# A transformer block with a Fourier layer on one core: two token tiles normalised on another engine, and the last sums of the MLP in three pieces

## The chip, the cores and the metric

The kernel runs on one core of a Trainium2 chip. The metric is the device time of one execution in microseconds; of the kernel before there are three runs, 2810.19, 2811.89 and 2812.22 us, median 2811.89 us. One more execution was recorded by the hardware profiler; every duration below is from it. The engines have short names in the profile: PE (TensorE, matrix products), PEld (its weight loads), DVE (VectorE), ACT (ScalarE), POOL (GpSimd) and SP (SyncE, which here only issues transfers). Each engine takes its own instructions in a fixed order; between engines, semaphores say when an operand is there.

## The reference

The input is x, 48 x 48 positions of 768 channels, which are 2304 tokens. Layer 0 is a transformer block, cut here to what matters:

```python
xn = layernorm(x, ln1_g, ln1_b)
qkv = xn @ qkv_w + qkv_b
out = softmax(q k^T * scale + rel_h + rel_w) v @ proj_w + proj_b     # 12 heads
x = x + out
xn2 = layernorm(x, ln2_g, ln2_b)
h = gelu(xn2 @ mlp_w1 + mlp_b1)                                      # 3072 wide
x = x + (h @ mlp_w2 + mlp_b2)
```

Layer 1 takes a two-dimensional Fourier transform of x over the 48 x 48 positions, multiplies the modes with small complex weights (8 blocks of 96 channels) in two steps with relu and soft shrinkage, transforms back and adds x. All data are float32.

## The kernel before

A tile of tokens is 128 tokens (one for each partition) by 768 channels; there are 18 of them. The stages follow each other on PE: layer norm and the products for q, k and v; attention; the projection; the MLP; the Fourier layer.

**The start.** `arrive(g)` loads three token tiles into one buffer `x3` (L403 to L406, one transfer on SP for each tile). Before the first product the first six tiles are normalised in place. `look_at(t)` (L410) takes mean and variance on DVE (two `bn_stats` L414, one `bn_aggr` L416) and the square root of the variance on ACT (L418). `normal(t)` (L421) takes the reciprocal on DVE (L424) and then, also on DVE, subtracts the mean and multiplies by the reciprocal (L426). The loop at L635 to L642 sets the order by hand for DVE, ACT and POOL: look at 0, look at 1, normalise 0, look at 2, normalise 1, normalise 2. Then `channels_first(0)` (L504) transposes the three tiles on PE (L510, in the order tile 0, 1, 2 for every 128 channels), scales them on DVE (L513) and ACT (L517), and PE goes on to the first products `plain_queries_and_keys` (L574). The load of the second set of weights (`weights_of` with `normalised[0]`, L379) is held back until tile 0 is normalised. Four POOL additions and subtractions (L166 to L169, from `left`) work on that load.

**The MLP.** Its products are done by Winograd's form of Strassen's scheme: seven products of half-size blocks in place of eight, at the price of sums of blocks before and after. Tokens go in three blocks `p` of 768 (two halves of G = 384), the 3072 hidden channels in 12 chunks `n` of 256 (two halves of 128). For each `(p, n)`:

- `hidden(p, n)` (L1332) makes the chunk of h: products on PE (L1343), sums on DVE (L1355), gelu on ACT (L1349). It is a generator that is advanced four times; in its last step `left` (L165 to L169) makes the sums of activations that the second product needs. With a11, a12, a21, a22 the blocks of h these are s1 = a21 + a22, s2 = s1 - a11, s4 = a12 - s2 in the buffer `hs`, and s3 = a11 - a21, which is written over a21 in `hT`. Each is one DVE instruction over 384 tokens.
- `added(p, n, i)` (L1386) makes the second product for 128 tokens of each half, i = 0, 1, 2: seven matmuls (L1408, then L1404 six times) into four PSUM banks `o0` to `o3`, each followed on DVE by an addition of the bank to `acc` or to the result in `main` (L1412 and L1406). The matmuls read, in this order, a11, s2, s3, s1, a12, a22, s4. For the last chunk of a block three more additions follow: one on DVE (L1420) and two on POOL (L1421, L1422).

In the loop at L1500 `added` of chunk n - 1 stands between the steps of `hidden` of chunk n, so that PE has products of one while DVE works for the other. After the last chunk of a block nothing of `hidden` is left: L1518 to L1521 run `added(p, 11, i)` for i = 0, 1, 2 one behind the other, for p = 0 and 1 with transposes between them (`turned`), for p = 2 with nothing between. `rows_forward(p)` (L1424) follows, the first step of the Fourier layer (L1436).

The order of PE, POOL and SP in this stage is the order in which the program issues (`in_order`), and so is that of DVE and ACT (`part_by_part`, L1497). What stands later in the text of the program stands later in the queue of its engine.

**The buffers.** `bias` (L1297) is a pool of constants that is placed ahead of the buffers for h, for the sums and for the weights.

Of the kernel before, what the change touches and what calls it, by code (L numbers as in the profile page):

```python
# [10 lines left out]
F32 = mybir.dt.float32  # L11
F32R = mybir.dt.float32r
I32 = mybir.dt.int32
AF = mybir.ActivationFunctionType
ALU = mybir.AluOpType
# [4 lines left out]
P = 128  # L20
HW = 48
T = HW * HW
# [7 lines left out]
TB = 768  # L30
G = 384
# [16 lines left out]
def block_then_afno(  # L48
# [27 lines left out]
    nc = tc.nc  # L76
# [40 lines left out]
    x1 = main.rearrange("p (t c) -> p t c", t=NT)  # L117
# [47 lines left out]
    def left(eng, a11, a12, a21, a22, s):  # L165
        eng.tensor_tensor(s[0], a21, a22, ALU.add)  # L166
        eng.tensor_tensor(s[1], s[0], a11, ALU.subtract)  # L167
        eng.tensor_tensor(s[2], a12, s[1], ALU.subtract)
        eng.tensor_tensor(a21, a11, a21, ALU.subtract)  # L169
# [30 lines left out]
    with ExitStack() as flag_scope:  # L200
# [12 lines left out]
        with ExitStack() as att:  # L213
# [121 lines left out]
            def queries_keys_values(qkv):  # L335
# [72 lines left out]
                normalised, looked_at = [], {}  # L408
# [12 lines left out]
                def normal(t):  # L421
                    x1 = arrived[t // 3][:, t % 3]
                    mv, rstd = looked_at.pop(t)
                    nc.vector.reciprocal(rstd, rstd)  # L424
                    normalised.append(
                        nc.vector.tensor_scalar(  # L426
                            x1, x1, mv[:, 0:1], rstd, ALU.subtract, ALU.mult
                        )
                    )

                def gathered(p):

# [182 lines left out]
                for p in range(T // TB):  # L615
                    work = [(0, pr) for pr in range(NC)] + [(1, i) for i in range(3)]
                    if p == 1:
                        work = work[NC:] + work[:NC]
                    elif p == 2:
                        work = work[:1] + work[NC:] + work[1:NC]  # L620
# [84 lines left out]
            with tc.manual_schedule(engines={mybir.EngineType.PE, mybir.EngineType.SP}):  # L705
# [161 lines left out]
                with tc.manual_schedule(  # L867
                    engines={mybir.EngineType.Activation, mybir.EngineType.DVE}
                ):
                    for pr in range(NC):  # L870
                        for c in range(T // G):
# [19 lines left out]
                            work = between(pr, c, acc)  # L891
# [109 lines left out]
        with tc.tile_pool(name="ps_flag", bufs=1, space=PSUM) as psum, tc.tile_pool(  # L1001
            name="ps_early", bufs=1, space=PSUM
# [55 lines left out]
        with tc.If(safe < 1):  # L1058
            with ExitStack() as att:
                xnT = main.rearrange("p (c t) -> p c t", c=NC)  # L1060
                with tc.tile_pool(name="g_ln1", bufs=3) as ln1, tc.tile_pool(
                    name="g_ps_ln1", bufs=2, space=PSUM
# [24 lines left out]
                for pr in range(NC):  # L1087
# [12 lines left out]
                    for g in range(T // G):  # L1100
                        kp = psum.tile([P, G], F32, name="g_kp", tag="m")
                        for c in range(NC):
# [5 lines left out]
                            bias=kb[0:64, pr : pr + 1], scale=HD**-0.5,  # L1108
# [18 lines left out]
                    for sg in range(T // SG):  # L1127
# [4 lines left out]
                        for i in range(2):  # L1132
                            qp = psum.tile([P, G], F32, name="qp", tag="m")
                            for c in range(NC):
# [6 lines left out]
                                bias=vec[0:64, V_QB + pr : V_QB + pr + 1],  # L1141
# [6 lines left out]
                        for i in range(2):  # L1148
                            hp = psum.tile([P, G], F32, name="g_hp", tag="m")
                            for r in range(8):  # L1150
                                h = sg * 16 + i * 8 + r
# [85 lines left out]
            with tc.tile_pool(name="g_ps_proj", bufs=2, space=PSUM) as psum, tc.tile_pool(  # L1237
                name="g_og", bufs=2
# [17 lines left out]
        with tc.tile_pool(name="ps_turn", bufs=4, space=PSUM) as psum_turn, tc.tile_pool(  # L1256
            name="ps_proj", bufs=1, space=PSUM
        ) as psum, tc.tile_pool(name="proj_late", bufs=2) as pl:
            hats, ogs = [], {EARLY: sums_of_outputs(pl, kept[EARLY])}
            for u in range(EARLY, PAIRS):  # L1260
# [5 lines left out]
                n = u - EARLY  # L1266
# [29 lines left out]
    with ExitStack() as mlp:  # L1296
# [7 lines left out]
        apart = mlp.enter_context(tc.tile_pool(name="apart", bufs=1))  # L1304
        apart.tile([P, 560], F32, name="apart")
        wpool = mlp.enter_context(tc.tile_pool(name="mlp_w", bufs=2))
        n_f = FF // FCH
        kept = {}

# [22 lines left out]
        def hidden(p, n):  # L1332

            a11, a12, a21, a22, ws, v, vs = ready_w.pop((p, n))
            h = hpool.tile([P, 2, TB], F32, name="hT")
            hs = hpool.tile([P, 3, G], F32, name="hs", bufs=1)
            kept[p, n] = h, hs, v, vs

            bank = [psum.tile([P, G], F32, name=f"h{i}") for i in range(4)]

            def product(i, a, b, start):
                for c in range(3):
                    nc.tensor.matmul(  # L1343
                        bank[i], a[:, c, :], b[:, c, :],
                        start=(start and c == 0), stop=(c == 2), skip_group_check=not start,
                    )

            def gelu(i, k, src):
                nc.scalar.activation(  # L1349
                    h[:, i, ts(k, G)], src, AF.Gelu, bias=col(V_B1 + 2 * n + i)  # L1350
                )

            def summed(src, other, name, bufs=2):
                t = upool.tile([P, G], F32, name=name, bufs=bufs)
                nc.vector.tensor_tensor(t, src, other, ALU.add)  # L1355
                return t

            b11, b21, t3, b22, t1, t2, t4 = parts_of_tokens(xt, xs)
            s1, s2, s4 = (ws[:, i] for i in range(3))
            product(0, a11, b11, True)  # L1360
            m1 = upool.tile([P, G], F32, name="m1")
            nc.scalar.copy(m1, bank[0])
            product(1, s2, t2, True)
            u = summed(bank[1], m1, "u")
            yield
            product(2, a21, t3, True)
            u7 = summed(bank[2], u, "u7")
            product(3, s1, t1, True)
            gelu(1, 1, summed(bank[3], u7, "c", 3))
            yield  # L1370
            product(0, a12, b21, False)
            gelu(0, 0, bank[0])
            product(2, a22, t4, False)
            gelu(1, 0, summed(bank[2], u, "c", 3))
            product(3, s4, b22, False)
            gelu(0, 1, summed(bank[3], u, "c", 3))
            yield
            left(
                nc.vector, h[:, 0, :G], h[:, 1, :G], h[:, 0, G:], h[:, 1, G:],
                [hs[:, i] for i in range(3)],  # L1380
            )
            yield

        acc = {}

        def added(p, n, i):  # L1386

            h, hs, v, vs = kept[p, n]
            bank = [psum.tile([P, CH], F32, name=f"o{k}") for k in range(4)]
            if n == 0:  # L1390
                acc[i] = upool.tile([P, CH], F32, name=f"acc{i}", bufs=1)
            a11, a12, s3, a22 = (
                h[:, f, ds(k * G + i * P, P)] for f, k in ((0, 0), (1, 0), (0, 1), (1, 1))
            )
            s1, s2, s4 = (hs[:, k, ts(i, P)] for k in range(3))
            b11, t3, b21, b22 = (v[:, f, ts(k, CH)] for f in range(2) for k in range(2))
            t1, t2, t4 = (vs[:, k] for k in range(3))
            t = 2 * (p * 3) + i
            x11, x12, x21, x22 = (
                x1[:, t + 3 * j, ts(k, CH)] for j in range(2) for k in range(2)  # L1400
            )

            def product(k, a, b, start, *into):
                nc.tensor.matmul(bank[k], a, b, start=start, stop=True, skip_group_check=not start)  # L1404
                for dst in into:
                    nc.vector.tensor_tensor(dst, bank[k], dst, ALU.add)  # L1406

            nc.tensor.matmul(bank[0], a11, b11, start=True, stop=True)  # L1408
            if n == 0:
                nc.vector.tensor_copy(acc[i], bank[0])  # L1410
            else:
                nc.vector.tensor_tensor(acc[i], bank[0], acc[i], ALU.add)  # L1412
            product(1, s2, t2, True, acc[i])
            product(2, s3, t3, True, x22)
            product(3, s1, t1, True, x22)
            product(0, a12, b21, False, x11)
            product(2, a22, t4, False, x21)
            product(3, s4, b22, False, x12)
            if n == n_f - 1:
                nc.vector.tensor_tensor(x21, x21, acc[i], ALU.add)  # L1420
                nc.gpsimd.tensor_tensor(x12, x12, acc[i], ALU.add)  # L1421
                nc.gpsimd.tensor_tensor(x22, x22, acc[i], ALU.add)  # L1422
# [61 lines left out]
        def turned(piece):  # L1484

            for i in range(4 * piece, 4 * piece + 4):
                j, c = divmod(i, NC)
                tp = psum.tile([P, G], F32, name="tp2", tag=f"h{i % 4}")
                for k in range(3):
                    nc.tensor.transpose(tp[:, ts(k, P)], hats[3 * j + k][:, ts(c, P)], ident)  # L1490
                nc.scalar.activation(
                    xt[:, c, ts(j, G)], tp, AF.Identity, bias=col(V_LN2B + c), scale=col(V_LN2G + c)
                )
# [6 lines left out]
        for p in range(T // TB):  # L1500
            for n in range(n_f):
                if (p, n) == (0, 2):
                    nc.sync.dma_start(out=b2, in_=mlp_b2[0, :].partition_broadcast(P))
                    nc.sync.dma_start(out=rows_dft, in_=c_rows)
                work = hidden(p, n)
                for i in range(3):
                    next(work)
                    if n:
                        added(p, n - 1, i)
                next(work)  # L1510
                if n < n_f - 1 and (p == 0 or n):
                    weights(p, n + 1)
                if p < 2 and 3 <= n < 9:
                    measured(p + 1, n - 3)
                if p < 2 and n > 8:
                    for i in range(2 * (n - 9), 2 * (n - 8)):
                        normalised(p + 1, i)
            for i in range(3):  # L1518
                if p < 2:
                    turned(i)  # L1520
                added(p, n_f - 1, i)  # L1521
            if p < 2:
                sums_of_tokens(xt, xs)
                for n in range(2):
                    weights(p + 1, n)
            rows_forward(p)
# [408 lines left out]
```

## Time and profile before

| | us |
|---|---|
| median of three runs | 2811.89 |
| the profiled execution, its own time | 2809.43 |
| its span | 2807.6 |
| PE busy | 2779.3 (99% of the span) |
| DVE busy | 1700.3 (61%) |
| ACT busy | 916.8 (33%) |
| POOL busy | 664.6 (24%) |
| first matmul starts (from the span's start) | 7.09 |
| last `added` of the MLP, first matmul | 2544.93 |
| first matmul of the last `rows_forward` | 2560.38 |

The profiled execution is 2.46 us under the median of the runs, and its span is 1.83 us under its own time. The granted clock of TensorE was 0.999 in it. A row of the timeline gives start, duration, engine, line, operation, output and inputs, shape, count, and in brackets how long the engine was idle before and what released it. Where a row has a count, the duration is that of the whole group. A matmul of float32 shows as two PE instructions in such a group.

### The profile page before, as it was taken

Reading aid. Unit: us, or ns where it says so; the run is one execution under the profiler, and the core shown is the slowest. Engines: PE = TensorE matmul, PEld = TensorE weight load, DVE = VectorE, ACT = ScalarE, POOL = GpSimd, SP = SyncE. Lnnn points to the kernel's source line nnn. Section 1 sums busy time; section 2 is a strip of 40 time slices with the busy share of each in tenths; the row PEclk is TensorE's granted clock in tenths of the full one; section 3 lists DMA queues with packets and bytes.
Section 4 is the critical chain, followed back from the end, with each engine's and each line's share of the span. In section 5 each row is a group of like instructions: output and inputs, shape, how many; then the busy total and the mean of one; then the engine's idle time right before and its main releaser. Section 6 shows DMA issues by size and latency. Waiting matters only on the chain. (4 is left out here: it accounts for less than half of the span.)

```text
span 2807.6 us, 40998 instructions
## 1 busy us (share of the span) xinstructions
PE 2779.3 (99%) x15765; PEld 1712.6 (61%) x15765; DVE 1700.3 (61%) x2504; ACT 916.8 (33%) x1457; POOL 664.6 (24%) x658
## 2 busy tenths in 40 slices
PE   8999999999999999999999999999999999999999
PEld 5555656656566566565556555555555555556888
DVE  4434245767676767676756566665666566566666
ACT  1101136656566666664501101121101211012432
POOL 2405010000000000000064332342232522322433
PEclk9999999999999999999999999999999999999999
DMA  5435385273663737546242112121121211114255
GB/s 180 160 109 168 97 158 113 56 136 66 104 129 62 132 63 120 107 73 101 84 168 79 52 67 67 45 102 57 45 68 52 97 54 63 50 56 123 64 152 158
DMA packets 218556, 269.39 MB, mean 96 GB/s; under 512 B 24772, under 2 KB 197180, under 8 KB 216816
## 3 DMA queue, kind: packets, MB, share of 16 engines
q1 hardware_dynamic: 217820, 266.15, 37.8%
q8 instruction: 127, 2.08, 0.3%
q14 instruction: 77, 0.63, 0.1%
q10 hardware_dynamic: 468, 0.33, 0.1%
q0 software_dynamic: 64, 0.20, 0.0%
HBM read 150.56 MB, written 52.32 MB: 72 GB/s over the span
## 5 line engine op out<-in xcount | busy, mean ns | idle before, releaser
L741 ACT ACTIVATE main<-sp 128x768 f32<-128x768 f32 x648 | 516.1, 812 | 34.7 <-PE sp L731 19.3
L885 DVE TENSOR_TENSOR pairs<-pairs,main 128x1536 f32<-128x1536 f32 x252 | 443.1, 1758 | 27.2 <-DVE pairs L885 0.9
L731 PE MATMUL sp<-terms,select 64*128 64x384 f32 x1296 | 412.0, 629 | 0.0
L1406 DVE TENSOR_TENSOR main<-o,main 128x384 f32<-128x384 f32 x540 | 299.7, 557 | 42.8 <-PE o L1404 0.5
L1343 PE MATMUL h<-shared,w 128*128 128x384 f32 x864 | 296.6, 486 | 0.7 <-POOL w2s L172 0.7
L722 PE MATMUL sp<-shared 64*128 64x384 f32 x1296 | 265.2, 485 | 1.6 <-ACT row_hi L246 1.0
L722 PE MATMUL sp<-qT,kT 64*128 64x384 f32 x1296 | 264.1, 484 | 0.0
L1343 PEld LDWEIGHTS h<-shared,w 128*128 128x128 f32 x864 | 163.9, 190 | 116.2 <-POOL w2s L172 1.3
L787 POOL TENSOR_TENSOR inverse<-inverse,rden 24x32 f32<-24x32 f32 x36 | 14.9, 415 | 925.8 <-DVE sums L786 886.5
L1343 PE MATMUL h<-shared,w1s 128*128 128x384 f32 x648 | 226.7, 486 | 0.0
L754 PE MATMUL op<-main,shared 128*64 128x384 f32 x1296 | 217.4, 488 | 0.0
L754 PE MATMUL op<-main,v 128*64 128x384 f32 x1296 | 216.4, 488 | 0.0
L1349 ACT ACTIVATE hT<-c,vec 128x384 f32<-128x384 f32 x108 | 66.4, 615 | 457.6 <-DVE c L1355 457.6
L885 DVE TENSOR_TENSOR pairs<-main 128x1536 f32<-128x1536 f32 x36 | 63.3, 1759 | 247.0 <-ACT main L741 247.0
L1355 DVE TENSOR_TENSOR c<-h,u 128x384 f32<-128x384 f32 x108 | 60.2, 558 | 218.4 <-PE h L1343 218.4
L731 PEld LDWEIGHTS sp<-terms,select 64*128 64x128 f32 x1296 | 125.3, 186 | 83.8
L1404 PE MATMUL o<-w2s,hs 128*128 128x384 f32 x432 | 174.9, 487 | 1.2 <-DVE hs L167 1.2
L1404 PE MATMUL o<-w,hT 128*128 128x384 f32 x432 | 175.1, 487 | 0.8 <-DVE hT L169 0.5
L1343 PEld LDWEIGHTS h<-shared,w1s 128*128 128x128 f32 x648 | 123.1, 190 | 85.9
L172 POOL TENSOR_TENSOR w2s<-w 128x384 f32<-128x384 f32 x36 | 36.0, 999 | 575.4 <-DMA w<-in_mlp_w_dram 347.2
L754 PEld LDWEIGHTS op<-main,v 128*64 128x64 f32 x1296 | 96.9, 137 | 92.7 <-issue 67.7
L553 PE MATMUL m<-main 128*128 128x384 f32 x462 | 150.6, 487 | 0.6 <-POOL main L167 0.6
(222 smaller groups left out, 4119.5 us busy)
## 6 DMA issues: line engine op xcount, KB each, us to landing
w<-in_mlp_w_dram SPq DMA_DIRECT2D x72, 768.0 KB
terms<-col_parts SPq DMA_DIRECT2D x432, 72.0 KB
terms<-row_hi SPq DMA_DIRECT2D x216, 72.0 KB
terms<-row_lo SPq DMA_DIRECT2D x216, 72.0 KB
main<-in_qkv_w_dram SPq DMA_DIRECT2D x36, 384.0 KB
z<-zt SPq DMA_DIRECT2D x48, 192.0 KB
x<-in_x_blocks_dram SPq DMA_DIRECT2D x18, 384.0 KB
q_d<-o SPq DMA_DIRECT2D x36, 192.0 KB
```

The lines of the kernel that those rows point to most:

```text
L172: eng.tensor_tensor(t[0], b12, b11, ALU.subtract)
L553: nc.tensor.matmul(bank, a[:, c, :], b[:, c, :], start=(first and c == 0), stop=(c == 2), skip_group_check=not first,)
L722: nc.tensor.matmul(sp[:, j, :G], kT[at, ts(kt, P)], qT[at, ts(c, G)], start=first, stop=not first,)
L731: nc.tensor.matmul(sp[:, j, :G], select[at, a % 2], ready[pr, c][at, a // 2, b], start=first, stop=not first,)
L741: nc.scalar.activation(p, sp[:, :, :G], AF.Exp, scale=HD**-0.5)
L754: nc.tensor.matmul(op[ts(j, 64)], v[:, kt, ts(j, 64)], exps[:, kt, j, :], start=(kt == 0), stop=(kt == NT - 1),)
L885: nc.vector.tensor_tensor(pairs, so_far, exps[:, ds(kt - 1, 2)], ALU.add)
L1343: nc.tensor.matmul(bank[i], a[:, c, :], b[:, c, :], start=(start and c == 0), stop=(c == 2), skip_group_check=not start,)
L1349: nc.scalar.activation(h[:, i, ts(k, G)], src, AF.Gelu, bias=col(V_B1 + 2 * n + i))
L1355: nc.vector.tensor_tensor(t, src, other, ALU.add)
L1404: nc.tensor.matmul(bank[k], a, b, start=start, stop=True, skip_group_check=not start)
L1406: nc.vector.tensor_tensor(dst, bank[k], dst, ALU.add)
```

## The change

Two places are changed.

1. In `normal(t)` the tiles 0 and 1 are normalised on ACT: DVE makes -mean * rstd (128 x 1) in the place of the variance, and ACT makes x * rstd + that, in place. ACT's order becomes: square root 0, square root 1, normalise 0, square root 2, normalise 1. Tiles 2 to 5 stay on DVE.
2. Three buffers `piece0` to `piece2` of 128 x 512 are added to the pool `bias`. For the very last chunk, (p, n) = (2, 11), the sums of activations are made in three pieces of 128 tokens, each in its own buffer with room for s1, s2, s4, s3. The generator stops after each piece: the first piece is made where all the sums were made before, the second between `added(2, 11, 0)` and `added(2, 11, 1)`, the third between `added(2, 11, 1)` and `added(2, 11, 2)`. Inside a piece the order is s1, s2, s3, s4. The matmuls of the last chunk read the pieces.

In the changed program the order of all other instructions is as before on every engine; DVE has the two normalisations replaced by two 128 x 1 operations and has twelve instructions over 128 tokens for four over 384.

```diff
@@ normal(t) @@
                     nc.vector.reciprocal(rstd, rstd)
-                    normalised.append(
-                        nc.vector.tensor_scalar(
+                    if t < 2:
+                        nc.vector.tensor_scalar(mv[:, 1:2], mv[:, 0:1], rstd, -1.0, ALU.mult, ALU.mult)
+                        last = nc.scalar.activation(
+                            x1, x1, AF.Identity, bias=mv[:, 1:2], scale=rstd
+                        )
+                    else:
+                        last = nc.vector.tensor_scalar(
                             x1, x1, mv[:, 0:1], rstd, ALU.subtract, ALU.mult
                         )
-                    )
+                    normalised.append(last)
@@ the MLP's pools @@
         wpool = mlp.enter_context(tc.tile_pool(name="mlp_w", bufs=2))
+        pieces = [bias.tile([P, 4, P], F32, name=f"piece{i}") for i in range(3)]
@@ hidden(p, n), last step @@
-            left(
-                nc.vector, h[:, 0, :G], h[:, 1, :G], h[:, 0, G:], h[:, 1, G:],
-                [hs[:, i] for i in range(3)],
-            )
-            yield
+            if (p, n) != (T // TB - 1, n_f - 1):
+                left(
+                    nc.vector, h[:, 0, :G], h[:, 1, :G], h[:, 0, G:], h[:, 1, G:],
+                    [hs[:, i] for i in range(3)],
+                )
+                yield
+            else:
+                for i in range(3):
+                    a11, a12, a21, a22 = (
+                        h[:, f, ds(k * G + i * P, P)] for f, k in ((0, 0), (1, 0), (0, 1), (1, 1))
+                    )
+                    s1, s2, s4, s3 = (pieces[i][:, k] for k in range(4))
+                    nc.vector.tensor_tensor(s1, a21, a22, ALU.add)
+                    nc.vector.tensor_tensor(s2, s1, a11, ALU.subtract)
+                    nc.vector.tensor_tensor(s3, a11, a21, ALU.subtract)
+                    nc.vector.tensor_tensor(s4, a12, s2, ALU.subtract)
+                    yield
@@ added(p, n, i) @@
-            s1, s2, s4 = (hs[:, k, ts(i, P)] for k in range(3))
+            if (p, n) != (T // TB - 1, n_f - 1):
+                s1, s2, s4 = (hs[:, k, ts(i, P)] for k in range(3))
+            else:
+                s1, s2, s4, s3 = (pieces[i][:, k] for k in range(4))
@@ the loop over blocks @@
             for i in range(3):
                 if p < 2:
                     turned(i)
+                elif i:
+                    next(work)
                 added(p, n_f - 1, i)
```

## The prediction

> **What bounds the kernel now.** I read the page's busy times first, then what PE waited for, then the timeline at the two places that the diff touches, and last the places where DVE and POOL work side by side.
>
> ```profile
> PE 2779.3 (99%) x15765; PEld 1712.6 (61%) x15765; DVE 1700.3 (61%) x2504; ACT 916.8 (33%) x1457; POOL 664.6 (24%) x658
> ```
>
> PE is the bound: 2779.3 of 2807.6 us. Only PE's 28 us of idleness can be won, and whatever makes PE idle longer is lost. PE's waits over the whole span:
>
> ```profile
> PE m L510 <- DVE x L426: 8.8, 3, 7.1
> PE m L970 <- DVEq L1058: 3.7, 1, 3.7
> PE o L1404 <- DVE hs L167: 1.2, 1, 1.2
> ```
>
> (total, times, longest.) The first row and the third lie where the change is made; a last one of 0.5 in three waits, for L169, belongs to the third. The timeline of the start:
>
> ```profile
> 6.95 1.01 DVE L414 BATCH_NORM_STATS2 stats<-x 128x6 f32<-128x384 f32 x2
> ...
> 8.27 0.68 DVE L426 TENSOR_SCALAR x<-x,mv,rstd 128x768 f32<-128x768 f32 x1
> ...
> 9.06 0.68 DVE L426 TENSOR_SCALAR x<-x,mv,rstd 128x768 f32<-128x768 f32 x1
> ...
> 9.79 3.60 PE L510 MATMUL m<-ident,x 128*128 128x128 f32 x16 [0.31 <-DVE x L426]
> ```
>
> DVE runs without a gap until tile 2 is normalised (9.74); PE's waits between 10 and 330 us are that row's 0.3 alone, so what is won ahead of 9.79 moves everything. The last group of the MLP:
>
> ```profile
> 2545.60 0.55 DVE L166 TENSOR_TENSOR hs<-hT 128x384 f32<-128x384 f32 x1
> ...
> 2546.89 0.88 PE L1404 MATMUL o<-w2s,hs 128*128 128x384 f32 x2 [1.16 <-DVE hs L167]
> ...
> 2550.61 0.81 PE L1404 MATMUL o<-w,hs 128*128 128x384 f32 x2
> ...
> 2551.26 0.81 PE L1408 MATMUL o<-w,hT 128*128 128x384 f32 x2
> ...
> 2551.93 0.55 DVE L1420 TENSOR_TENSOR main<-main,acc 128x384 f32<-128x384 f32 x1
> 2552.09 1.24 POOL L1421 TENSOR_TENSOR main<-main,acc 128x384 f32<-128x384 f32 x1 [26.67 <-DVE main L1406]
> ```
>
> PE's step is 0.645 us a matmul (2550.61 to 2551.26). The reader is to see two things: PE waits once, at s2; and DVE is behind PE at every seam: L1420 of group 0 starts 1.32 us after that group's last matmul, when PE is two matmuls into group 1. Today nothing of group 1 needs DVE at that moment. And POOL works just then.
>
> **Part 1, the start.** Removed from DVE: two 0.68 us operations. Added: two of 128x1, priced by the reciprocal L424 (0.11 to 0.15 us). The first takes the place at 6.36; the statistics of tile 2 can then start at about 6.46 instead of 6.95, their aggregate (L416, now at 8.00) at 7.51. Reciprocal 1 follows at 7.64, the second 128x1 at 7.78; the root of tile 2 on ACT at 7.75 (0.24 after the aggregate, as now) until 8.05, reciprocal 2 at 8.08, normalise 2 at 8.27 until 8.95. ACT: normalise 1 is queued behind the root of tile 2; it starts 0.2 after that (L418 to L579, 17.79 to 17.99), at 7.95. Its length: L487 (128x768, one column operand) takes 0.936, and a second column costs 0.671 (L517) - 0.578 (L562) = 0.093: 1.03 us, until 8.98. PE transposes tile 1 at 9.03 (0.05 later; tile 1 is now ready at 8.95 and transposed at 9.01) and tile 2 at about 9.28, in place of 9.79: 0.5 us won. Unknown is when tile 2 lands: no wait shows before 6.95, so it is there by then. Were it only just there, the chain ends 0.49 - 0.14 later and about 0.1 is left; if tile 1 follows faster, 0.6. I take 0.5: the 1.18 MB of the first three tiles have passed by 5.5 us, and tile 0 was used 0.8 us after its bytes had passed, which puts tile 2 at 6.3.
>
> What moves with it: normalise 0 ends on ACT at about 7.7 instead of 7.04, so the weight load L379 is issued 0.6 later on SP; nothing else waits in SP then, and the queue's engines have tokens to carry until 14, so it lands at 15.1 as before and its user on PE comes at 30.7. DVE's tiles 3 to 5 come 0.5 earlier, run into POOL's L166 and lose that again; tile 5 is ready at 20.2 as now, PE needs it at about 20.8. ScalarE keeps its one table (one load ahead of the roots and the identities of the start). [...]
>
> **Part 2, group 0.** Now s1, s2, s3 cost 0.55 each from 2545.60, s2 ends at 2546.75 and PE goes at 2546.89. The fixed part of such an operation follows from 0.549 (384 elements) and 0.945 (768, L1573): 1.03 ns an element and 0.15 fixed, so 0.285 for 128. s1 2545.60, s2 2545.92 to 2546.20, matmul 2 at 2546.34; s3 (now third, and in its own buffer) ends at 2546.4, before matmul 3 needs it at 2546.99. Matmul 4 starts at 2547.63 in place of 2548.68: 1.05 us won.
>
> **Part 3, groups 1 and 2.** Pieces 1 and 2 stand in DVE's queue behind all seven evictions of the group before and L1420. Call M the start of a group's last matmul. Its eviction starts at M + 0.85 (2555.12 to 2555.97), L1420 at M + 1.32, the next DVE operation at M + 1.79 (L1412 at 2552.40 follows 0.47 behind L1420). PE wants s2 for the second matmul of the next group at M + 1.29, before s1 has begun. Without anything else: s1 at M + 1.79, s2 at M + 2.11 until M + 2.39, matmul at M + 2.52 (0.12 to 0.14, as at 2546.75): PE idles 1.23 us, twice. That is the lower bound.
>
> But L1421 and L1422 run on POOL at exactly that time, and s1 and s2 read both operands from SBUF, as POOL does. How such pairs go:
>
> ```profile
> 2220.16 8.38 DVE L184 TENSOR_TENSOR shared<-shared 128x1152 f32<-128x1152 f32 x4
> 2221.07 2.11 POOL L1422 TENSOR_TENSOR main<-main,acc 128x384 f32<-128x384 f32 x1
> 2223.14 2.11 POOL L166 TENSOR_TENSOR w1s<-w 128x384 f32<-128x384 f32 x1
> ```
>
> Four L184 take 8.38 beside POOL, where three take 4.21 with POOL idle (23.41); POOL's take 2.11 instead of 1.00. They go one after another in turn. How long POOL holds DVE off: at 17.82 L426 lasts 1.11 instead of 0.68, so it began at 18.25, 0.73 after POOL's L168 (17.52); I count 0.75. L1421 itself lasts 1.24, that is, it begins 0.24 late, 0.40 after L1420 did. So, in the changed kernel: L1421 begins in effect at M + 1.72 and holds until M + 2.47; s1 goes then, ends at M + 2.76; L1422 is issued 0.97 after L1421, M + 2.69, just ahead of s2 (M + 2.80), and holds until M + 3.44; s2 ends at M + 3.72, matmul 2 at M + 3.84: idle 2.55 us. If POOL holds its whole 1.00, s2 ends 0.42 later: 2.97, the upper bound. I take 2.55, twice 5.1, because it comes from the row with the same two engines; 1.23 and 2.97 give the range. [...]
>
> The last group's evictions stand to its last matmul as now, and the chain into L1436 and the Fourier layer moves as a whole. The MLP's tiles move up in SBUF by 6 KB a partition; no transfer of SP waits for anything new.
>
> **Sum.** -0.5 - 1.05 + 5.1 = +3.55 us. The profiled execution, 2809.43, would become 2813.0; it stood 2.46 under the median, so the median becomes 2811.89 + 3.5 = 2815.4 us. About 0.2% (5.6 us) is what a measurement of this kernel can tell from no change; the forecast is slower, but inside it.
>
> **Rivals.**
> - No turn-taking: the pieces run at full speed beside POOL. -0.5 - 1.05 + 2.46 = +0.9: 2812.8. For it: L1420 itself keeps its 0.548 beside L1421. Against: it began first there, and L184 doubled.
> - The gain stands: s2 of pieces 1 and 2 is ready in time, -1.55: 2810.3. It decides if s2 ends by M + 1.17; against it, the eviction that precedes it in the queue starts at M + 0.85 and L1420 still comes between. Slower turns into faster from an idle time under 0.78 a group.
> - Slower beyond 0.2%: the moved weight tiles lie where a buffer of the projection was, and their first load, now issued at 1513.19, waits for its last reader, PE at 1543.8. A load takes 4.4 us to POOL's first use (1556.62 to 1561.05), against PE's start at 1544.70: +3.5 to +4.5, in all +7.5: 2819.4. It decides if that load is issued after 1535. Against: SP's waits are the old ones.
> - The change does nothing at the start: tile 2 lands at 6.95. That leaves +3.9.
>
> **Numbers.** Turn-taking (idle 1.9 to 2.97 a group) 0.67; no turn-taking 0.21; gain stands 0.04; late weights 0.04; start without gain, else as forecast, 0.04. The range: no turn-taking gives 2812.8, the upper bound 2.97 with 0.1 at the start gives +4.8, 2816.7; each widened by the runs' own spread of about 1.3: 2811.4 to 2818.0. Slower by over 0.2%: the late weights and a tenth of turn-taking with the spread on top, 0.12; faster by over 0.2% asks -5.6, which no case gives: 0.02; within: 0.86.
>
> **What the profile after would show.** Start: two 1.0 us ACT operations, PE's long run of transposes from about 9.3. Group 0: PE's wait for s2 about 0.6 instead of 1.16. Groups 1 and 2: PE waiting for DVE's piece 1.2 to 3.0 us each, and under turn-taking a row of s1 near 1 us, not 0.28, or idle of that length, and L1422 above 1.00. L1436 4 us later against the start of PE's run. I would be wrong if the pieces' s2 ended before PE's first matmul of the group, or if PE waited for weights at 1544.

## The result, and the profile after

The changed kernel takes 2816.04 us (median of 22 runs, 2811.47 to 2820.99) beside 2810.68 us of the kernel before on the same chip (22 runs, 2806.50 to 2814.15). The ratio is 1.0022, 95% interval [1.0016, 1.0028]: slower by 6.2 us, 4.5 to 7.9. (The ratio is not the quotient of the two medians, which is 1.0019 or 5.4 us; that lies inside the interval.) The forecast was +3.55 us and 2815.4 us. The direction and the mechanism in the MLP were right. The gain at the start did not show, the loss is about 1.75 times what was summed, and the rest of this text is about the missing part.

The profiled execution of the changed kernel took 2816.98 us, its span 2815.1 (before: 2809.43 and 2807.6). The page's busy times:

```profile
PE 2783.3 (99%) x15765; PEld 1715.3 (61%) x15765; DVE 1704.6 (61%) x2512; ACT 920.1 (33%) x1459; POOL 665.5 (24%) x658
```

The waits of PE in the same profile (total, times, longest):

```profile
PE m L515 <- ACT x L427: 8.8, 2, 7.7
PE o L1425 <- DVE piece L1397: 5.6, 3, 2.5
PE m L975 <- DVEq L1063: 3.6, 1, 3.6
```

PE's wait for the sums of activations, 1.2 us in one place before, is now 5.6 us in three. PE is also *busy* 4.0 us longer, with the same 15765 instructions. That is the first sign that it ran slower somewhere. The timeline of the changed kernel's last three groups (start, duration, engine, line, and in brackets the idle time ahead and its releaser):

```profile
2546.49 0.88 PE L1425 MATMUL o<-w2s,piece 128*128 128x384 f32 x2 [0.62 <-DVE piece L1397]
...
2551.11 0.55 DVE L1441 TENSOR_TENSOR main<-main,acc 128x384 f32<-128x384 f32 x1
2551.27 1.24 POOL L1442 TENSOR_TENSOR main<-main,acc 128x384 f32<-128x384 f32 x1 [25.63 <-DVE main L1427]
2551.57 1.08 DVE L1396 TENSOR_TENSOR piece<-hT 128x128 f32<-128x128 f32 x1
2552.47 1.04 POOL L1443 TENSOR_TENSOR main<-main,acc 128x384 f32<-128x384 f32 x1
2552.69 0.97 DVE L1397 TENSOR_TENSOR piece<-piece,hT 128x128 f32<-128x128 f32 x1
...
2553.71 1.65 PE L1425 MATMUL o<-w2s,piece 128*128 128x384 f32 x2 [2.47 <-DVE piece L1397]
...
2555.16 1.49 PE L1425 MATMUL o<-w,piece 128*128 128x384 f32 x2
...
2557.26 0.81 PE L1425 MATMUL o<-w,hT 128*128 128x384 f32 x2
```

Group 0 waits 0.62 us. At the seam to group 1, s1 (L1396) and s2 (L1397) last 1.08 and 0.97 us beside POOL's two additions, and PE is idle for 2.47 us. Then something unforeseen: the matmul that follows takes 1.65 and the next but one 1.49, where the same matmul takes 0.81 from 2557.26 on. Stretches of 3.4 us of the changed kernel show why (length, then busy time and instructions of PE, PEld, DVE, ACT and POOL, then the granted clock of PE, DMA share, GB/s):

```profile
2550.00:2553.40 3.40, 1.24 (x4) 0.38 (x2) 3.28 (x5) 0.00 (x0) 2.13 (x2) 1.00 0.00 0
2553.40:2556.80 3.40, 3.09 (x5) 1.85 (x6) 1.81 (x6) 0.00 (x0) 0.11 (x1) 0.50 0.00 0
2556.80:2560.20 3.40, 3.21 (x10) 1.52 (x8) 2.92 (x6) 0.00 (x0) 0.17 (x1) 1.00 0.00 0
2560.20:2563.60 3.40, 1.13 (x4) 0.73 (x5) 3.23 (x7) 0.00 (x0) 2.07 (x2) 1.00 0.00 0
2563.60:2567.00 3.40, 3.40 (x7) 1.86 (x6) 1.59 (x4) 0.00 (x0) 0.00 (x0) 0.50 0.00 0
```

With each of the two long waits PE was granted half its clock for 3.41 us (0.50 from 2553.38 and from 2563.62). From the first matmul of the last `added` to the first of the Fourier layer it is 23.17 us (2545.06 to 2568.23) instead of 15.45 (2544.93 to 2560.38): +7.7. Against the kernel before, group 0 wins 0.95, each of the two waits delays its matmul by 2.63, and the matmuls behind them lose 1.62 and 1.80 more, of which about 1.6 each is the half clock (a run without half clock, below, loses 0.1 there). The 2.63 is 0.16 more than the idle time of 2.47, since a matmul shows 0.81 us in the profile and the next would have followed after 0.645.

### The profile page after: what moved, and what is told of

Read it like the earlier page. It is cut to its first block, busy times and chain, and to the rows that moved or that the text cites. A ratio compares the mean times of both kernels' runs of the same rounds, so it can differ in the third digit from the quotient of the medians.

```text
span 2815.1 us, 41013 instructions
## 1 busy us (share of the span) xinstructions
PE 2783.3 (99%) x15765; PEld 1715.3 (61%) x15765; DVE 1704.6 (61%) x2512; ACT 920.1 (33%) x1459; POOL 665.5 (24%) x658
## 5 line engine op out<-in xcount | busy, mean ns | idle before, releaser
L172 POOL TENSOR_TENSOR w2s<-w 128x384 f32<-128x384 f32 x36 | 36.0, 1000 | 575.5 <-DMA w<-in_mlp_w_dram 400.8
L759 PEld LDWEIGHTS op<-main,shared 128*64 128x64 f32 x1296 | 96.3, 137 | 89.4 <-issue 64.4
```

Source lines behind the costliest of these rows:

```text
L759: nc.tensor.matmul(op[ts(j, 64)], v[:, kt, ts(j, 64)], exps[:, kt, j, :], start=(kt == 0), stop=(kt == NT - 1),)
```

## The experiments

The tail's length in the table is that stretch, from the first matmul of the last `added` to the first of `rows_forward`, from one profile of each kernel. Waits are PE's idle times for the sums of activations, in the order of the timeline, those under 0.2 us left out; the 0.57 of e11 is for an accumulator instead. "Half" counts the 3.41 us stretches at half clock inside the tail. Each ratio is to runs of the kernel before on the same chip, whose medians were 2810.68 (changed), 2809.97 (e1 to e4), 2809.57 (e5 to e8) and 2810.33 (e9 to e11): medians of different groups are compared by their ratios.

| kernel | median us | ratio [95%] | tail us | waits us | half |
|---|---|---|---|---|---|
| before | 2810.68 | 1 | 15.45 | 1.16 | 0 |
| changed | 2816.04 | 1.0022 [1.0016, 1.0028] | 23.17 | 0.62, 2.47, 2.46 | 2 |
| e1 start alone | 2810.15 | 0.9998 [0.9989, 1.0007] | 15.45 | 1.15 | 0 |
| e2 pieces alone | 2818.20 | 1.0026 [1.0017, 1.0036] | 19.97 | 0.62, 2.47, 2.47 | 0 |
| e3 POOL later | 2812.53 | 1.0007 [0.9998, 1.0016] | 18.62 | 0.62, 1.80, 1.79 | 0 |
| e8 no POOL at the seam | 2811.10 | 1.0003 [0.9994, 1.0012] | 17.03 | 0.62, 1.00, 1.00 | 0 |
| e6 idle without POOL | 2815.81 | 1.0020 [1.0010, 1.0030] | 23.36 | 0.62, 2.47, 2.47 | 2 |
| e4 PE filled, 3 matmuls | 2816.33 | 1.0021 [1.0012, 1.0030] | 19.98 | 0.62, 0.54, 0.54 | 0 |
| e9 PE filled, 2 matmuls | 2814.04 | 1.0011 [1.0002, 1.0020] | 19.98 | 0.62, 1.18, 1.18 | 0 |
| e11 pieces all at once | 2810.28 | 0.9999 [0.9990, 1.0008] | 15.74 | 0.62, 0.57 | 0 |
| e7 whole sums on POOL | 2812.67 | 1.0012 [1.0003, 1.0021] | 18.60 | 1.63, 1.11 | 1 |
| e5 pieces on POOL | 2807.89 | 0.9990 [0.9981, 0.9999] | 13.64 | none | 0 |
| e10 as e5, without the start | 2808.89 | 0.9991 [0.9982, 1.0000] | 13.64 | none | 0 |

### The two parts apart

The first part alone, on the kernel before (e1), has the hunk in `normal(t)` and nothing else (shortened):

```diff
+                    if t < 2:
+                        nc.vector.tensor_scalar(mv[:, 1:2], mv[:, 0:1], rstd, -1.0, ALU.mult, ALU.mult)
+                        last = nc.scalar.activation(x1, x1, AF.Identity, bias=mv[:, 1:2], scale=rstd)
+                    else:
+                        last = nc.vector.tensor_scalar(...)
```

> Only the start: tiles 0 and 1 normalised on ScalarE, the MLP as in the kernel before. By the forecast's first part the third tile is transposed about 0.25 to 0.5 us earlier than 9.79 us, and the whole is 0.5 us shorter, which is below what the runs can tell (ratio 0.9998). [...]

Measured: 0.9998 [0.9989, 1.0007], no difference. In its profile tile 2 was transposed at 9.37 instead of 9.79, but the third PE instruction of the first product (L574 before) started at 14.00, 0.12 later than before (13.88), and PE reached L553 (L558 there) at 30.82 instead of 30.69. That is within 0.2 us: nothing of the 0.42 is left at 30 us. Why is not shown.

The second part alone (e2) is the rest of the diff, `normal(t)` as before:

```diff
-                    if t < 2:
-                        nc.vector.tensor_scalar(mv[:, 1:2], mv[:, 0:1], rstd, -1.0, ALU.mult, ALU.mult)
-                        last = nc.scalar.activation(
-                            x1, x1, AF.Identity, bias=mv[:, 1:2], scale=rstd
-                        )
...
```

> Only the three pieces, the start as in the kernel before. If the loss is all in the MLP's last chunk: PE waits about 2.5 us for s2 of pieces 1 and 2 and then runs some of the following matmuls at 1.28 us a step instead of 0.645; the first matmul of the last row transform comes about 7.8 us later than in the kernel before, relative to the first matmul of the last group, and the time is 5 to 8 us above before. If the start contributes to the loss, this kernel is clearly faster than the changed one.

Measured: 1.0026 [1.0017, 1.0036]; the whole loss is in the pieces. By luck the profiled execution (2810.54 us, the fastest of its runs) had the same three waits to a hundredth and no half clock in the tail. Its stretches of 3.4 us, with the same columns:

```profile
2546.30:2549.70 3.40, 2.31 (x8) 1.03 (x6) 3.16 (x6) 0.00 (x0) 1.06 (x1) 1.00 0.00 0
2549.70:2553.10 3.40, 2.02 (x6) 1.25 (x7) 3.15 (x7) 0.00 (x0) 1.17 (x2) 1.00 0.00 0
2553.10:2556.50 3.40, 2.76 (x9) 1.33 (x7) 3.05 (x7) 0.00 (x0) 0.61 (x1) 1.00 0.00 0
2556.50:2559.90 3.40, 1.57 (x5) 1.04 (x6) 3.17 (x6) 0.00 (x0) 1.62 (x2) 1.00 0.00 0
2559.90:2563.30 3.40, 3.40 (x14) 1.64 (x15) 3.03 (x6) 0.00 (x0) 0.16 (x1) 1.00 0.00 0
```

The waits of 2.47 us end at 2551.08 and 2558.33. In the two rows that share the first one PE is busy 2.31 and 2.02 of 3.40 us, in the row with most of the second 1.57; in the changed kernel it was 1.24 and 1.13 ahead of half clock. Why the clock stayed at 1.00 in this execution is not shown. The tail is 4.5 us longer than before, not 7.7.

### What lengthens s1 and s2: POOL

In e3 and e8 POOL's six last additions (L1442, L1443) are taken out of the groups and issued after them; e3 issues those of group 0 first, e8 those of group 2 first, so that in e8 none can start before the last group has ended. The diff of e8 (e3 has `late[::2] + late[1::2]`):

```diff
-        acc = {}
+        acc, late = {}, []
...
-                nc.gpsimd.tensor_tensor(x12, x12, acc[i], ALU.add)
-                nc.gpsimd.tensor_tensor(x22, x22, acc[i], ALU.add)
+                for dst in (x12, x22):
+                    if p < 2:
+                        nc.gpsimd.tensor_tensor(dst, dst, acc[i], ALU.add)
+                    else:
+                        late.append((dst, acc[i]))
...
+            for dst, other in late[::-2] + late[-2::-2]:
+                nc.gpsimd.tensor_tensor(dst, dst, other, ALU.add)
```

> The changed kernel, but the six last additions on GpSimd for the third token block are issued behind the three groups instead of inside each. Theory (DVE's s1 and s2 take turns with GpSimd's additions, and a long idle halves PE's clock): s1 and s2 of pieces 1 and 2 take 0.28 us each instead of 1.08 and 0.97, PE waits 1.2 us twice instead of 2.47, the clock stays at 1.0, and the row transform starts about 1.6 us later than before instead of 7.8; the time is 1 us above before. Rival (the place in DVE's queue alone makes the wait): 2.4 us waits and the slow steps stay, 5 to 8 us above before.

> The changed kernel with the six last additions of GpSimd (x12 and x22 of the three groups) issued after the groups, those of the last group first, so that none can run while the pieces of groups 1 and 2 are made. Theory (turn-taking): s1 and s2 fall from 1.08 and 0.97 us to 0.28 each, the waits in groups 1 and 2 from 2.47 to about 1.2 us each; and as the idle time is shorter, no 3.4 us at half clock follow; the tail about +1.7 us against before, with the start about +1.2 us, a ratio of 1.0004. Rival (the first sum waits for the end of VectorE's own sums, not for GpSimd): the waits stay at 1.8 us or more and the ratio at 1.001 to 1.002.

Measured in e3: POOL, free to go ahead, made the first addition of each group as soon as its operands were there, at the seam. s1 stayed at 1.08 us, s2 fell to 0.29, the waits to 1.80 and 1.79. The expected 1.2 was wrong because only one of two POOL additions had been moved away. The timeline of e3 at the seam to group 1:

```profile
2551.83 1.24 POOL L1549 TENSOR_TENSOR main<-main,acc 128x384 f32<-128x384 f32 x1 [25.53 <-DVE main L1427]
2552.13 1.08 DVE L1396 TENSOR_TENSOR piece<-hT 128x128 f32<-128x128 f32 x1
2553.25 0.29 DVE L1397 TENSOR_TENSOR piece<-piece,hT 128x128 f32<-128x128 f32 x1
2553.59 0.91 PE L1425 MATMUL o<-w2s,piece 128*128 128x384 f32 x2 [1.80 <-DVE piece L1397]
```

In e8 both are gone; its timeline at the same seam:

```profile
2549.08 0.55 DVE L1441 TENSOR_TENSOR main<-main,acc 128x384 f32<-128x384 f32 x1
2549.54 0.28 DVE L1396 TENSOR_TENSOR piece<-hT 128x128 f32<-128x128 f32 x1
2549.86 0.29 DVE L1397 TENSOR_TENSOR piece<-piece,hT 128x128 f32<-128x128 f32 x1
...
2550.21 0.91 PE L1425 MATMUL o<-w2s,piece 128*128 128x384 f32 x2 [1.00 <-DVE piece L1397]
```

s1 and s2 last 0.28 and 0.29, PE waits 1.00. So a POOL addition beside s1 and one beside s2 cost the wait 0.8 and 0.67 us (1.00, 1.80, 2.47). What is left, 1.00 us twice, is the place in DVE's queue: L1441 still stands ahead of s1, and POOL is not busy. With both gone the time is the old one within what can be measured (1.0003).

### What halves the clock: the idle time

e6 is e8 with two clearings of the buffer `hs`, which the last chunk does not use, ahead of pieces 1 and 2. They hold DVE for 1.25 us; POOL does nothing then.

```diff
+                    if i:
+                        nc.vector.memset(hs, 0.0)
+                        nc.vector.memset(hs[:, 0, :192], 0.0)
```

> The kernel with no GpSimd addition at the seams, but with 1.25 us of clearing of an unused buffer on VectorE ahead of pieces 1 and 2: TensorE is idle again for about 2.45 us in groups 1 and 2, with GpSimd out of it. [...] Rival (the half clock belongs to GpSimd and VectorE running together, not to the idle time): steps stay at 0.645 us and the time is 2.5 us above the run without the clearing.

Measured: waits of 2.47 and 2.47 us, and half clock after both. The stretches of e6, columns as above:

```profile
2550.90:2554.30 3.40, 0.93 (x4) 0.29 (x2) 2.98 (x9) 0.00 (x0) 0.00 (x0) 1.00 0.00 0
2554.30:2557.70 3.40, 3.40 (x6) 1.89 (x7) 1.82 (x5) 0.00 (x0) 0.00 (x0) 0.50 0.00 0
2557.70:2561.10 3.40, 2.97 (x10) 1.43 (x8) 2.70 (x5) 0.00 (x0) 0.00 (x0) 1.00 0.00 0
2561.10:2564.50 3.40, 1.36 (x4) 0.87 (x5) 2.95 (x8) 0.00 (x0) 0.00 (x0) 1.00 0.00 0
2564.50:2567.90 3.40, 3.40 (x7) 1.84 (x6) 1.82 (x4) 0.00 (x0) 1.21 (x2) 0.50 0.00 0
```

POOL's column is 0.00 in the first four rows: the half clock comes with PE's idle time and without POOL, and the rival (DVE and POOL together) falls by the profile. The median is 4.7 us above that of e8, where the longer waits explain 2 x 1.47 = 2.9; about 1.8 us are left for the clock, less than the 2.5 or more that I had expected for it. By time alone it could not be told whether there was half clock: by the intervals the difference to e8 is uncertain by almost 4 us.

The opposite test: leave the sums as late as they are and shorten PE's idle time with matmuls into an unused accumulator (work nobody needs; the result is untouched). e4 has three of them in each of groups 1 and 2, e9 two:

```diff
+            if (p, n) == (T // TB - 1, n_f - 1) and i:
+                spare = psum.tile([P, CH], F32, name="spare", tag="h0")
+                for _ in range(3):
+                    nc.tensor.matmul(spare, a11, b11, start=True, stop=True)
```

> The changed kernel with three more matmuls (0.645 us each) into an unused PSUM bank behind the first matmul of groups 1 and 2, that is, in the time in which PE waits for s2; their result is not used. DVE's and GpSimd's work is unchanged, so s2 is ready when it was. Theory (the slow steps are the granted clock falling after PE has been idle): the matmuls behind the wait run at 0.645 us a step, and the row transform starts 3 to 3.5 us earlier than in the changed kernel, about 4.4 us later than in the kernel before; the time is 2 to 4 us below the changed kernel. Rival (the steps are slow because of the pieces' buffers or of the banks): steps of 1.28 us stay and the time is that of the changed kernel.

> The changed kernel with two products into an unused accumulator inside each of the two waits of groups 1 and 2 (work that nobody needs; the sums' places on VectorE stay as they are), so that TensorE is idle for about 1.2 us there and not 2.47. Theory (half clock follows from the idle time): no half clock in the tail, the tail +4.4 us against before, the median 1 to 2.5 us below that of the changed kernel, a ratio of 1.0014. Rival (the filling costs as much as it saves, as the run with three products suggested): the ratio is 1.002 or more.

Measured: both profiles have no half clock in the tail and 19.98 us for it, as e2 without half clock. The timeline of e9 in group 1, with s2 as late as before and the steps behind it at 0.645 us:

```profile
2550.05 1.45 PE L1433 MATMUL spare<-w,hT 128*128 128x384 f32 x4
2552.68 0.91 PE L1425 MATMUL o<-w2s,piece 128*128 128x384 f32 x2 [1.18 <-DVE piece L1397]
2553.43 0.81 PE L1425 MATMUL o<-w,piece 128*128 128x384 f32 x2
```

e9's median is 2.0 us below that of the changed kernel, as expected (by the ratios, each to its own runs of the kernel before, 1.0011 against 1.0022; the intervals overlap). e4's median did not fall (1.0021), against what was expected. Its +5.9 us has an interval of 3.4 to 8.4, which holds the tail's 4.5, so in time e4 is inconclusive. Its profiled execution is 6.8 us longer than that of e2, which has the same tail: from the first matmul of the Fourier layer on, e4 falls behind by 1.3 us at a wait for a transfer at 2577, and by 4.7 more in the last rows, where PE is idle for 3.33 us at 2796.79 and the 96 instructions behind it take 10.66 us, while 64 of the same shape ahead of it took 5.42. With one profile it is not shown that this is why its median stayed.

The mean granted clock is known for every run, not for the profiled one alone. Turned into time at half clock it is 11.5 us a run in the mean of the changed kernel's 22 runs and 12.4 in the 10 of e2, against 7.6 in the 90 runs of the kernel before that went with the experiments. In e4 it is 7.7 and in e9 6.1, back at the level of before; in e6 it is 9.4 against 5.1 in e8. (The standard error of each mean is 0.4 to 2.0 us.) So the changed kernel spends about 4 us more at half clock, which costs about 2 us of time with PE busy, and the filling takes that away in the runs too.

### Where the pieces could stand

e11 keeps the three pieces on DVE, in their own buffers, but issues all twelve sums ahead of group 0:

```diff
                     nc.vector.tensor_tensor(s4, a12, s2, ALU.subtract)
-                    yield
+                yield
...
-                elif i:
-                    next(work)
```

> The changed kernel with its three pieces still on VectorE and in buffers of their own, but all twelve sums issued one behind the other ahead of the first group, none between the groups. Theory (what costs is the place of pieces 1 and 2 behind the seam's own sums in VectorE's queue): twelve sums of about 0.25 us take 3.0 us where the four whole ones took 2.2, the first product that waits still starts about 1 us earlier than before, no wait for a piece in groups 1 and 2, no half clock in the tail; VectorE, which in the kernel before is busy nearly all of each 4.5 us group, begins to empty the accumulators up to 0.8 us later, so between 0 and -1.0 us in the tail, -0.6 taken, and a ratio of 0.9997 (0.9990 to 1.0003). Rival (VectorE becomes the bound of the tail): TensorE waits for accumulators (o behind VectorE's sums) by 1 us or more and the time is at or above that of the kernel before.

Measured: 0.9999 [0.9990, 1.0008]. s2 of group 0 is as early as in the changed kernel (wait 0.62) and groups 1 and 2 wait for no piece, but DVE comes to the accumulators later. The timeline of e11 in group 0:

```profile
2546.10 0.28 DVE L1399 TENSOR_TENSOR piece<-hT,piece 128x128 f32<-128x128 f32 x1
2546.30 0.55 DVE L1433 TENSOR_TENSOR acc<-o,acc 128x384 f32<-128x384 f32 x1
...
2547.00 0.88 PE L1425 MATMUL o<-w,hT 128*128 128x384 f32 x2 [0.57 <-DVE acc L1433]
2547.43 2.77 DVE L1427 TENSOR_TENSOR main<-o,main 128x384 f32<-128x384 f32 x5
2548.03 0.91 PE L1425 MATMUL o<-w2s,hT 128*128 128x384 f32 x2 [0.15 <-DVE main L1427]
```

The tail is 15.74, 0.3 longer than before where 0.6 shorter was expected: from the fourth matmul of group 0 on, PE's steps are 1.38, 1.03, 0.75 and 0.67 us instead of 0.645, in all 1.25 more, which takes the 0.95 back. The rival of that expectation, that PE waits for accumulators and the tail gains nothing, is what happened; the idle time itself is 0.72, less than the 1 us that it named.

e7 leaves the four sums whole and moves them to POOL (with the start's part); e5 moves the twelve small ones there, all ahead of group 0; e10 is e5 without the start's part.

```diff
@@ e7, on the kernel before @@
-                nc.vector, h[:, 0, :G], h[:, 1, :G], h[:, 0, G:], h[:, 1, G:],
+                nc.gpsimd if (p, n) == (T // TB - 1, n_f - 1) else nc.vector,
+                h[:, 0, :G], h[:, 1, :G], h[:, 0, G:], h[:, 1, G:],
@@ e5, on the changed kernel @@
-                    nc.vector.tensor_tensor(s1, a21, a22, ALU.add)
+                    nc.gpsimd.tensor_tensor(s1, a21, a22, ALU.add)
...
-                    yield
+                yield
...
-                elif i:
-                    next(work)
```

> The kernel before with the start's part, and with the four last sums of activations left whole (384 tokens) and moved to GpSimd; no pieces. By GpSimd's addition of 128 x 384 at about 1.00 us the second sum is ready about 2 us after the last GELU, near 2543.7 us, and the third near 2544.7 us, well ahead of the second product of the first group at 2546.3 us. Theory: no wait for the sums, the same gain in the tail as the pieces on GpSimd (-1.8 us) and a ratio near 0.9992; the pieces then buy nothing that another engine does not. Rival (four whole additions on GpSimd delay its first addition of group 0, and a group waits for it): a wait of 0.5 to 1 us of TensorE in the seam to group 1, and the gain is half gone.

> The changed kernel with the twelve sums of 128 tokens made on GpSimd, all at once after the last GELU, instead of on VectorE one group ahead of each turn. In the changed kernel's profile GpSimd does nothing between about 2525 us and its first addition at the group's end, so the first piece should be ready near 2543.6 us and the third near 2546. Theory (the cost of the change is where the second and third piece stand in VectorE's queue, behind sums that wait for TensorE's own results): no wait of TensorE for a piece in any of the three groups, steps of 0.645 us throughout, no half clock in the tail; the tail about 1.8 us shorter than in the kernel before; with the start's part at -0.1 to -0.4 us the time is -1.5 to -2.5 us, a ratio near 0.9992. Rival (smaller products of pieces, or their buffers, cost time by themselves): the tail stays at +2 us or more though no wait is seen.

> The kernel before with the twelve sums of 128 tokens on GpSimd ahead of the first group, without the start's part. Theory: the tail alone gives -1.6 to -1.8 us, a ratio of 0.9994; the start's part adds -0.2 to -0.5 us on average, less than this measurement can tell, so it is the same as with the start's part within 1 us. [...]

e7 is slower (1.0012 [1.0003, 1.0021]), against the expectation. Its timeline in group 0:

```profile
2544.04 1.00 POOL L166 TENSOR_TENSOR hs<-hT 128x384 f32<-128x384 f32 x1 [19.82 <-PE o L1409]
...
2546.16 0.91 PE L1409 MATMUL o<-w2s,hs 128*128 128x384 f32 x2 [1.63 <-POOL hs L167]
...
2548.19 1.56 PE L1409 MATMUL o<-w,hT 128*128 128x384 f32 x2 [1.11 <-POOL hT L169]
```

POOL could not start when the last gelu was done. s1 writes into `hs`, and PE was still reading the sums of the chunk before from it: the bracket names PE, and the start is 2544.04. I had overlooked that buffer. Two waits, 1.63 and 1.11, ended at 2546.16 and 2548.19, and PE's next steps were 1.35, 1.28 and 1.10 us instead of 0.645: half clock, as behind the waits of the changed kernel (step 1.28 from 2564.10).

The timeline of e5 at the same place:

```profile
2542.22 0.46 POOL L1396 TENSOR_TENSOR piece<-hT 128x128 f32<-128x128 f32 x1 [16.41 <-ACT hT L1355]
2542.76 0.46 POOL L1397 TENSOR_TENSOR piece<-piece,hT 128x128 f32<-128x128 f32 x1
...
2546.06 0.81 PE L1425 MATMUL o<-w2s,piece 128*128 128x384 f32 x2
```

The pieces have buffers of their own, so POOL starts when the last gelu ends, s2 is ready near 2543.2, and at 2546.06 PE goes on without a wait, in all three groups. The tail is 13.64, 1.82 shorter than before (expected 1.8), in e5 and in e10 alike. The ratios are 0.9990 [0.9981, 0.9999] and 0.9991 [0.9982, 1.0000]. By its ratio e5 is about 2.8 us faster than the kernel before (by the medians 1.7), the only version here whose interval lies wholly below 1; by the ratios it beats the changed kernel by some 9 us. The tail's 1.82 lies inside that interval (0.3 to 5.3). The products of pieces and their buffers are the same in e5 as in the changed kernel, so neither costs time by itself. The start's part adds nothing that shows (0.0001 between e5 and e10); a gain of 1.5 us or more from it is not supported, though the intervals are too wide to exclude it.

## Why the prediction was right, and where its sum was short

- **The start, -0.5: failed as a gain.** The order was as described: two ACT operations of 1.03 us, DVE's statistics of tile 2 earlier. The profile of the changed kernel:

```profile
6.37 0.22 DVE L426 TENSOR_SCALAR mv<-mv,rstd 128x1 f32<-128x1 f32 x1
6.62 1.03 ACT L427 ACTIVATE x<-x,mv,rstd 128x768 f32<-128x768 f32 x1
6.64 1.02 DVE L414 BATCH_NORM_STATS2 stats<-x 128x6 f32<-128x384 f32 x2
...
8.21 1.03 ACT L427 ACTIVATE x<-x,mv,rstd 128x768 f32<-128x768 f32 x1
...
8.46 0.68 DVE L431 TENSOR_SCALAR x<-x,mv,rstd 128x768 f32<-128x768 f32 x1
...
9.29 1.11 PE L515 MATMUL m<-ident,x 128*128 128x128 f32 x4 [1.13 <-ACT x L427]
```

  The step that was mis-sized is "two of 128x1, priced by the reciprocal (0.11 to 0.15 us)": they last 0.21 to 0.22, and every following step is 0.2 later than summed (statistics 6.64, not 6.46; normalise 2 at 8.46, not 8.27). Tile 2 is transposed at 9.56, 0.23 earlier than before and not 0.5. Over all profiles the ten kernels with this part have 9.37 to 9.95, mean 9.55, the three without it 9.73 to 9.94, mean 9.82: 0.27 won. And "what is won ahead of 9.79 moves everything" is not borne out. PE's transposes follow each other by 0.213 us up to 12.84 in the kernel before and 12.76 in the changed one, and by 0.109 at 21.1 to 23.0; the first full clock in the records is at 13.19 before and at 13.86 in the changed kernel; at the third PE instruction of the first product the ten stand at 13.94 in the mean and the three at 13.90, and at the first instruction of L553 (by the lines of before) at 30.86 and 30.72. No gain shows there, among profiles that differ by over 1 us. Whether the first matmul, which is 0.6 later with ACT (7.70 for 7.09), moves the first grant is not settled by these runs.
- **Group 0, -1.05: right,** measured 0.95 in the changed kernel (wait 0.62 for "about 0.6"; the small sums last 0.28 for 0.285).
- **Groups 1 and 2, idle 2.55 each: right.** The prediction counted from the step of 0.645, and so counted it was 2.63 (2.47 and 2.46 of idle time in the profile). The case without turn-taking, 1.23, is 1.16 in e8 counted alike (1.00 of idle time); s1 "near 1 us" was 1.08. L1422, now L1443, was "above 1.00" with 1.04, and the two took turns. The upper bound of 2.97 does not come out of its steps: with a hold of 1.00 for 0.75 they give 2.80, or 3.12 if the second addition begins only when s1 has ended; the measured 2.63 is below both. The 2.63 is nearer to the hold of 0.75 that a row of the trace gave.
- **The missing term: the granted clock.** "Three groups, two waits of 2.55" was priced as idle time alone, and the sum assumed 0.645 us a matmul behind it. In the profile of the changed kernel two times 3.41 us at half clock added 3.2 us to the tail of e2, 1.6 each. The whole sum, then: -0.95, +2 x 2.63 and a remainder of +0.2 make the 4.5 us of e2's tail; the clock adds nothing in e2 and 3.2 in the changed kernel. Half clock followed four of the six waits of 2.46 or 2.47 us in the profiles of the changed kernel, e2 and e6: 2 x 4/6 x 1.6 = 2.1 us on average, an estimate from three profiles; the granted clock of all runs gave about 2. With the start at nothing, 4.5 + 2.1 = 6.6, against 6.2 measured (4.5 to 7.9).
- **The evidence was in the profile of the kernel before,** in the wait of 3.7 us that was listed and passed over because the change does not touch it:

```profile
1467.30:1470.70 3.40, 0.58 (x2) 0.48 (x3) 0.10 (x1) 0.00 (x0) 0.23 (x1) 1.00 0.01 5
1470.70:1474.10 3.40, 3.40 (x6) 1.69 (x6) 3.40 (x8) 0.26 (x1) 0.00 (x0) 0.50 0.00 0
```

  PE is busy 0.58 of 3.40 us, and the next stretch is at 0.50. The same wait, 3.6 to 3.8 us long, stands in all thirteen profiles; in that of the changed kernel (3.64 us, until 1469.43) the granted clock is 0.50 from 1467.94 for 6.83 us.
- **The rivals.** No turn-taking (+0.9) falls in the changed kernel; its wait appears in e8, where POOL is out of the way. The gain stands (-1.55) falls: s2 of pieces 1 and 2 is late by 2.63. Late weights: PE's wait near 1544 us (for L172) is 0.70 in both profiles. Nothing of the list had a price for a slower clock, and so the chance given to slower by over 0.2%, 0.12, looks too low for a ratio that stands at 1.0022. That the median, 2816.04, is so near the forecast 2815.4 is luck: these runs' median of the kernel before, 2810.68, lies 1.2 us under the 2811.89 that the sum started from. From 2811.89 the ratio 1.0022 would have led to 2818.1, just past the end of the range.

## What to carry to other kernels

Cutting an operation into pieces helped here only the piece that kept its old place in the queue; for each later piece, list what now stands ahead of it on its engine and what the neighbour that lengthened it here does at that moment (s1 took 1.08 us beside POOL's additions, 0.28 without), or give the pieces to an engine that is idle, into buffers that nobody still reads. And price idle time of PE by more than its length: add the chance of half clock behind it (here about 1.6 us each, behind four of six waits of 2.46 or 2.47 us). Last, look for a gain again further on: the 0.42 us that e1 won ahead of PE's first full clock were gone at 30 us, and the 1.8 us of e11 at the last rows.

## What the runs showed of the hardware that was not expected

- **Half clock behind a wait of 2.47 us.** In the changed kernel's profile the granted clock was 0.50 for 3.41 us with each of the waits of 2.47 and 2.46 us; in e6 it was 0.50 behind both, too, and in e2 behind none, with waits of the same length. What decides between executions with equal waits was not found.
- **The last rows' wait differs between executions.** Seven of the thirteen profiles show PE idle for 1.66 to 3.33 us ahead of the final products whose rows come back from DRAM, the other six at most 1.34 us there. In e11, which reached the Fourier layer 1.8 us ahead of the kernel before, this is where the lead went, by its timeline:

```profile
2795.26 1.14 PE L1760 MATMUL rps<-zl,shared 100*64 100x192 f32 x8 [1.98 <-issue]
```

  It appears in e1 too, whose only edit is at the start. What makes the difference was not found. It may be part of why executions of one kernel lie 3 to 10 us apart, but there is one profile of each kernel, and that is not shown.
